# One block of attention and gated FFN on one core: the product with V goes first in its step, the eighth output unit moves to step 6, and five x buffers

## The chip, the cores and the metric

The kernel runs on one core of a Trainium2 chip. A core has five engines that run their own instruction streams and meet at semaphores: TensorE (PE, matrix products into PSUM), VectorE (DVE), ScalarE (ACT), GpSimd (POOL) and SyncE (SP), which here only issues DMAs. The metric is the time of one execution in microseconds (us), lower is better; before the change the median of three runs is 1512.0 us (1510.33 to 1512.47).

## The reference, cut to what matters

```python
# x [2, 1024, 512]; 16 heads of size 128; FFN width 1365
def attn(x):
    q, k, v = (einsum('bsd,hed->bhse', x, W) for W in (W_Q, W_K, W_V))
    scores = where(causal, -1e9, einsum('bhse,bhme->bhsm', q, k) / sqrt(128))
    z = einsum('bhsm,bhme->bhse', softmax(scores), v)
    return einsum('bhse,hde->bsd', z, W_O)
def ffn(x):                       # w1q, w3q, w2q: weights rounded to -s, 0, +s
    return (silu(x @ w1q.T) * (x @ w3q.T)) @ w2q.T
x = x + layernorm(attn(layernorm(x)))
x = x + layernorm(ffn(layernorm(x)))
```

All is float32. Layernorm is over the last axis, and s is the mean of the absolute weights.

## The kernel before, in words

**Stages.** Attention of batch 0 and then of batch 1 fills the time to about 1270 us; the FFN follows. The heads of both batches are counted through: head n runs from 0 to 31, batch b is n // 16. Two heads make a pair g = n // 2, whose V and output weights are handled together; j = n % 2 tells the two apart.

**Steps.** Each head has eight steps i = 0 to 7, one for each tile of 128 queries, 256 steps in all. The last head takes its query tiles in the order 4 to 7, 0 to 3. A step puts this work on TensorE, in this order:
- up to two *units* from the list `fill[i]` (L860);
- if it is a product step, the *product with V* (`values`, L864, matmul at L650): probabilities, transposed, times V for two query tiles. Products m = 0 to 3 of a head are due at its steps 3, 5, 7 and at step 2 of the next head;
- the rest of the units (L867);
- the scores (`scores`, L556) of the query tile three steps ahead.

Units are: a half of the next head's Q or K projection (`query_key_unit`, L471 and L478, 12 matmuls), a quarter of the next pair's V (`value_unit`, L499, 24 matmuls), an output unit, which multiplies the last pair's z with W_O for one token tile (`output_units`, L519, 6 matmuls), a block unit, which transposes a normalised x tile of batch 1 (`block_unit`, L403), and in the last heads transposes for the FFN (L256) and FFN units (`early_hidden`, L318). Output units come in even heads: three at step 0, then one at each of steps 1, 4, 5, 6 and 7. V units come in odd heads, at steps 0, 1, 6 and 7.

**One chain per pair of query tiles.** Scores go to PSUM; VectorE masks the diagonal (L561) and takes the maximum (L565); ScalarE takes the exponential (L572) and, after VectorE's reciprocal (L577), scales it (L578); VectorE turns 32x32 blocks (L604). SP writes the blocks to DRAM ("hop", L615) and reads them back in four DMAs as `pt` (L631), which completes the transpose; the product needs these reads. ScalarE reads the product out twice (L662), VectorE and GpSimd make its low and difference forms (L667, L670).

**Split matmuls.** Projections and output units work on a leading, a low and a difference form of both factors. They write two PSUM tiles, main and diff. ScalarE scales main out (L454 for Q, K and V) and VectorE combines it with diff (L458 for q, L456 for k and v; L530 and L533 for output units, which add into `acc`). Weight forms are made by ScalarE (L439), GpSimd (L440) and VectorE (L446).

**PSUM.** The pool `ps_m` has four tiles that are handed out in turn: two for each projection, V or output unit, one for a product or a transpose. The pool `ps_s` has two, for scores; the transposes of the first batch use it too.

**Order.** The code fixes the order of TensorE's work with `past(newest[0])`. On the other engines a planner orders what the code leaves open; `behind(...)` puts weight forms and side work behind marked instructions. Each engine then runs its stream in that order. The lists `side` hold work beside the steps: loads for the statistics (L148, L354), x loads and normalisation for the second batch (`block_load` L380, `normal_unit` L388), rounding of the FFN weights (L199 to L219), and the middle of the block (L273 to L291). These tiles come from `xpool`.

**Start.** Tiles of x are normalised (L123 on VectorE, L388 on ScalarE), transposed (L403), and split (L407, L408, L409). `busy` (L703) adds transposes of an identity, of no use to the result.

Of the kernel before, what the change touches and what calls it, by code (L numbers as in the profile page):

```python
# [35 lines left out]
def sandwich_kernel(  # L36
# [30 lines left out]
    N = 2 * G  # L67
# [54 lines left out]
    def normalise(dst, src, mv, r, t):  # L122
        return nc.vector.tensor_scalar(  # L123
            dst, src, mv[:, t, 0:1], r[:, t : t + 1], ALU.subtract, ALU.mult
        )
# [212 lines left out]
    with ExitStack() as att:  # L338
# [4 lines left out]
        vpool = att.enter_context(tc.tile_pool(name="v", bufs=2))  # L343
        zpool = att.enter_context(tc.tile_pool(name="z", bufs=ZB))
        qpool = att.enter_context(tc.tile_pool(name="q", bufs=2))
        xpool = att.enter_context(tc.tile_pool(name="x", bufs=3))
        ps_s = att.enter_context(tc.tile_pool(name="ps_s", bufs=2, space=PSUM))


# [28 lines left out]
        def block_load(b, t):  # L378
            normal[b, t] = xt = xpool.tile([P, D], FP, name="xt")
            nc.sync.dma_start(xt, x[b, ts(t, P), :])  # L380

        def normal_unit(b, t):
            if b == 0:
                normal[b, t] = acc[:, t, :]
            xt = normal[b, t]
            if b == 0 and t % 2 == 1:
                return normalise(xt, xt, mv_in[b], r_in[b], t)
            return nc.scalar.activation(  # L388
                xt, xt, AF.Identity, scale=r_in[b][:, t : t + 1],
                bias=shifts[b][:, t : t + 1],  # L390
            )

        def block_unit(b, t):
            k, tl = divmod(t, QT)
            if tl == 0:
                xs[b, k] = [xblocks.tile([P, NC, TB], FR, name="xb") for _ in range(3)]
            xt = normal[b, t]
            if b == 0:
                ps = ps_s.tile([P, NC, P], FP, name="tr", tag="s_ps")
            else:  # L400
                ps = ps_m.tile([P, NC, P], FP, name="tr", tag="mm")
            for c in range(NC):
                newest[0] = nc.tensor.transpose(ps[:, c, :], xt[:, ts(c, P)], ident)  # L403
            lead, low, diff = (form[:, :, ts(tl, P)] for form in xs[b, k])
            eng = nc.vector if b == 0 and tl >= QT // 2 else nc.gpsimd
            return (
                nc.scalar.mul(lead, ps, LEAD / T12),  # L407
                nc.vector.scalar_tensor_tensor(low, lead, -T12, ps, ALU.mult, ALU.add),  # L408
                eng.tensor_tensor(diff, lead, low, ALU.subtract),  # L409
            )  # L410
# [271 lines left out]
        @contextmanager  # L682
        def past(*instructions):
            with ExitStack() as order:
                for i in instructions:
                    order.enter_context(tc.issue_after(i.ins))
                yield
# [10 lines left out]
        def busy(times):  # L698
            with ExitStack() as order:
                if newest[0] is not None:  # L700
                    order.enter_context(past(newest[0]))
                for _ in range(times):
                    newest[0] = nc.tensor.transpose(idle, ident, ident)  # L703
# [4 lines left out]
        with past(*done):  # L708
            for kind in range(2):
                lead_and_low(kind, 0, EVERY, first=True)  # L710
            blocks = []
            for t in range(QT):
                blocks.append(block_unit(0, t))
                if t % 2 == 1:
                    busy((8, 3)[t // 2])
        lead, low, diff = blocks[-1]
        with past(diff):
            for kind in range(2):
# [12 lines left out]
        side = [[] for _ in range(N * NT)]  # L731
        at = 0

        def two_steps_each(pairs, at):
            for first, then in pairs:
                side[at].append(first)
                side[at + 2].append(then)
                at += 2
            return at

        for k in range(3):
            pairs, total, last = mean_abs_units(k, xpool)
            at = two_steps_each(pairs, at)
            side[at + 1].append(total)
            side[at + 3].append(last)
        at = two_steps_each([stats_units(t) for t in range(NT)], at)
        side[at + 1].append(lambda: std_unit(1, 0, NT))

        block_at = 2 * (NP - 1) * NT + 5
        assert at + 1 < block_at - 3  # L750
        for t in range(NT):
            side[block_at - 3 + t].append(lambda t=t: block_load(1, t))
            side[block_at - 2 + t].append(lambda t=t: normal_unit(1, t))
        at += (1 - at) % 4 + 4
        for stages in ternary_steps(qpool):
            for later, stage in zip((0, 2, 3, 4), stages):
# [56 lines left out]
        for n in range(N):  # L813
            g, j = divmod(n, 2)
            b, pr = divmod(g, NP)

            fill = [[] for _ in range(NT)]

            def put(steps, units):
                for i, u in zip(steps, units):  # L820
                    fill[i].append(u)

            if n + 1 < N:
                units = [
                    lambda k=k, kind=kind: query_key_unit(n + 1, kind, k)()
                    for k in range(2)
                    for kind in range(2)
                ]
                late = {2 * NP - 1: (6, 7), N - 2: (5, 5)}.get(n, (5, 6))
                put((3, 4) + late, units)  # L830
            if j == 1 and g + 1 < G:
                units = [lambda u=u: value_unit(g + 1, u) for u in range(QT)]
                put((0, 1, 6, 7) if n != 2 * NP - 1 else (0, 1, 5, 6), units)
            if n == 0:
                put((1, 2), [lambda u=u: value_unit(0, u) for u in (2, 3)])
            if j == 0 and g > 0:
                outs = output_units(g - 1)
                put((0, 0, 0, 1, 4, 5, 6, 7), outs)
            for t in range(NT):
                if divmod(block_at + t, NT)[0] == n:  # L840
                    put([(block_at + t) % NT], [lambda t=t: block_unit(1, t)])
            for t in range(QT):
                if divmod(split_at + t, NT)[0] == n:
                    put([(split_at + t) % NT], splits[t][2:])
            if n == N - 1:
                put((2, 4, 6), [lambda f=f: early_hidden(f) for f in range(EARLY)])
            for i in range(NT):
                idx = n * NT + i
                with behind("turn", of=idx + 1):
                    if n + 2 < N and i > 5:  # L850
                        load_raw(i - 6, n + 2)
                    if j == 0 and g + 1 < G and i == 1 + (n == 0):
                        load_raw(2, g + 1)
                    if j == 1 and i == 1:
                        load_raw(3, g)
                    if n == N - 2 and i >= NT - EARLY:
                        f = i - NT + EARLY
                        load_t13(f, wpool.tile([P, 2, D], FR, name=("va", "vd", "vl")[f]))
                todo = fill[i]
                for u in todo[:2]:  # L860
                    with past(newest[0]):
                        u()
                rest = None
                if idx in product:  # L864
                    with past(newest[0]):
                        rest = values(*product.pop(idx))
                for u in todo[2:]:  # L867
                    with past(newest[0]):
                        u()

                with behind("max", "half", "exp", of=idx + 1):
                    if n + 1 < N and i in (2, 3):
                        difference_form(i - 2, n + 1, EVERY)
                    if n + 1 < N and i in (1, 2):
                        lead_and_low(i - 1, n + 1, EVERY)
                    at = g + 1 - j
                    form_step = i - 3 - (n == 0)
                    if at < G and form_step in (0, 1):
                        lead_and_low(2 + j, at, (FRONT, BACK)[form_step])
                    if at < G and form_step in (2, 3):  # L880
                        difference_form(2 + j, at, (FRONT, BACK)[form_step - 2])
                with past(newest[0]):
                    look(idx + AHEAD)
                if rest:
                    with behind("max"):
                        rest()
                if idx + 2 < len(order):
                    with behind("max"):
                        turn(*order[idx + 2])
                        if idx + 3 == len(order):  # L890
                            bring(*next(iter(blocks_of)))
                with behind("max", "half", "turn"):
                    for u in side[idx]:
                        u()
        outs = output_units(G - 1)
# [7 lines left out]
    with ExitStack() as ffn:  # L903
# [4 lines left out]
        xpool = ffn.enter_context(tc.tile_pool(name="xf", bufs=3))  # L908
# [208 lines left out]
```

## Time and profile before

| what | value |
|---|---|
| median of three runs | 1512.0 us (1510.33 to 1512.47) |
| the profiled execution | 1511.27 us |
| its span, first to last instruction | 1509.5 us |
| granted TensorE clock over the span | 0.997 |
| busy: PE, DVE, ACT, POOL | 98%, 72%, 53%, 27% |
| HBM traffic | 174 GB/s over the span |

All places in time below are microseconds from the start of the span. PE is TensorE's matmuls, PEld its weight loads. A row of a group or of the timeline gives engine, line, operation and tiles (out<-in). In the list of waits, an entry "A <- B" means that A's engine stood idle before A and that B ended it; then come the total, how often, and the longest. Brackets in the timeline give the idle time before an instruction and what ended it. A DMA's row shows the issue by SP; the trace also holds when it landed.

### The profile page before, as it was taken

To read this page: it belongs to the slowest core of one execution; us is meant where nothing else is said; L and a number is where in the kernel's file an instruction comes from. 1 tells how busy PE (TensorE), PEld (TensorE's weight loads), DVE (VectorE), ACT (ScalarE), POOL (GpSimd) and SP (SyncE) were. 2 spreads that over 40 slices of the span, in tenths; PEclk is the share of its full clock that TensorE was granted. 3 is DMA by queue.
4 is the path that set the end of the run, shared out by engine and by line. 5 is a ranking of instruction groups with operands and counts; after the bars stand their busy time and mean duration, and the time that the engine had idled before them with its cause. 6 is when DMAs were issued, how large, how long until landed. Compare 5 with 4: busy or idle time off the path is not lost.

```text
span 1509.5 us, 21335 instructions
## 1 busy us (share of the span) xinstructions
PE 1475.6 (98%) x7061; PEld 1184.9 (78%) x7061; DVE 1080.6 (72%) x2123; ACT 792.7 (53%) x1566; POOL 404.3 (27%) x472
## 2 busy tenths in 40 slices
PE   8999999999999999999999999999999999999997
PEld 6778888887878787777778787878787877888885
DVE  7767686878786878787777777777777776664444
ACT  4656555555555555666664555555555464444332
POOL 3222222222223333434433333333322110210010
PEclk9999999999999999999999999999999999999999
DMA  3666767676666675758866666666665677530200
GB/s 123 194 194 186 195 184 200 185 202 184 201 191 172 181 206 183 205 166 249 238 200 190 195 192 196 195 195 189 179 179 166 181 216 228 176 102 19 91 28 29
DMA packets 179894, 263.57 MB, mean 175 GB/s; under 512 B 19188, under 2 KB 120564, under 8 KB 175688
## 3 DMA queue, kind: packets, MB, share of 16 engines
q1 hardware_dynamic: 179784, 262.20, 59.5%
q8 instruction: 57, 0.93, 0.3%
q14 instruction: 53, 0.43, 0.1%
HBM read 160.43 MB, written 101.71 MB: 174 GB/s over the span
## 4 chain that ended last, share of the span: by engine, by line
PE 66%; issue 10%; DVE 9%; DMA 7%; ACT 5%; POOL 2%; SPq 1%; DVEq 0%; POOLq 0%; ACTq 0%
PE mm L650 11%; PE mm L471 10%; PE mm L318 10%; PE s_ps L556 10%; PE mm L499 8%; PE mm L519 6%; PE yp L933 5%; PE mm L478 5%; DVE nm L565 3%; DMA hop<-blocks 2%; ACT p_sb L572 2%; DMA wqk<-wk 2%; ACT p_sb L578 1%; POOL kl L440 1%; DVE blocks L604 1%
## 5 line engine op out<-in xcount | busy, mean ns | idle before, releaser
L572 ACT ACTIVATE p_sb<-s_ps,nm 128x128 f32<-128x128 f32 (+7 forms) x256 | 190.0, 742 | 367.3 <-DVE nm L565 360.8
L556 PE MATMUL s_ps<-k,q 128*128 128x512 f32 (+3 forms) x768 | 289.7, 486 | 0.7 <-ACT p_sb L572 0.7
L650 PE MATMUL mm<-pt,v_sb 128*128 128x256 f32 (+1 forms) x1280 | 271.7, 359 | 11.3 <-ACT q L454 3.7
L650 PEld LDWEIGHTS mm<-pt,v_sb 128*128 128x128 f32 x1280 | 238.1, 190 | 48.8 <-ACT q L454 6.2
L578 ACT ACTIVATE p_sb<-p_sb,ri 128x128 f32<-128x128 f32 (+7 forms) x256 | 197.7, 773 | 33.0 <-DVE ri L577 30.5
L565 DVE TENSOR_REDUCE nm<-s_ps 128x1 f32<-128x128 f32 (+7 forms) x256 | 193.7, 757 | 7.1
L604 DVE STREAM_TRANSPOSE blocks<-p_sb 128x128 f32<-128x128 f32 (+7 forms) x256 | 197.1, 770 | 1.2 <-ACT p_sb L578 0.9
L556 PEld LDWEIGHTS s_ps<-k,q 128*128 128x128 f32 x768 | 132.3, 190 | 69.4 <-issue 61.4
L670 POOL TENSOR_TENSOR zd<-za,zl 128x256 fp32r<-128x256 f32 x128 | 94.7, 739 | 328.0 <-DVE zl L667 319.7
L561 DVE TENSOR_TENSOR s_ps<-s_ps,causal 128x128 f32<-128x128 f32 x256 | 75.4, 295 | 136.1 <-PE s_ps L556 135.6
L499 PE MATMUL mm<-va,xb 128*128 128x256 f32 x512 | 158.5, 310 | 0.0
L499 PE MATMUL mm<-vd,xb 128*128 128x256 f32 x512 | 144.9, 283 | 0.9 <-POOL xb L409 0.9
L499 PE MATMUL mm<-vl,xb 128*128 128x256 f32 x512 | 144.6, 282 | 0.0
L471 PE MATMUL mm<-xb,qa 128*128 128x512 f32 x256 | 119.6, 467 | 1.0 <-ACT xb L407 1.0
L471 PE MATMUL mm<-xb,ka 128*128 128x512 f32 x256 | 112.3, 439 | 0.0
L499 PEld LDWEIGHTS mm<-vl,xb 128*128 128x128 f32 x512 | 97.7, 191 | 7.1 <-issue 4.1
L499 PEld LDWEIGHTS mm<-va,xb 128*128 128x128 f32 x512 | 97.7, 191 | 7.1 <-issue 3.9
L471 PE MATMUL mm<-xb,ql 128*128 128x512 f32 x256 | 101.7, 397 | 0.0
L471 PE MATMUL mm<-xb,kl 128*128 128x512 f32 x256 | 100.7, 393 | 0.1
L499 PEld LDWEIGHTS mm<-vd,xb 128*128 128x128 f32 x512 | 97.7, 191 | 1.1 <-POOL xb L409 1.1
L601 POOL MEMSET blocks<- 128x128 f32 x128 | 26.2, 205 | 263.1 <-DMA hop<-blocks 185.2
L533 DVE TENSOR_TENSOR acc<-acc,mm 128x512 f32<-128x512 f32 x128 | 86.1, 683 | 12.7 <-ACT acc L528 5.4
(162 smaller groups left out, 2777.3 us busy)
## 6 DMA issues: line engine op xcount, KB each, us to landing
hop<-blocks SPq DMA_DIRECT2D x32, 1024.0 KB, 4.5
pt<-hop SPq DMA_DIRECT2D x128, 256.0 KB, 6.2
hop<-blocks SPq DMA_DIRECT2D x32, 768.0 KB, 3.3
pt<-hop SPq DMA_DIRECT2D x128, 192.0 KB, 3.8
hop<-blocks SPq DMA_DIRECT2D x32, 512.0 KB, 3.2
pt<-hop SPq DMA_DIRECT2D x128, 128.0 KB, 3.2
wqk<-wq SPq DMA_DIRECT2D x32, 256.0 KB, 5.2
wqk<-wk SPq DMA_DIRECT2D x32, 256.0 KB, 6.6
```

The costliest lines, as they stand in the source:

```text
L318: newest[0] = nc.tensor.matmul(ps[:fl, :], lhsT=t[:, c, :], rhs=bl[k][:, c, :], start=(c == 0 and k == 0), stop=(c == NC - 1 and k == 1),)
L471: newest[0] = nc.tensor.matmul(main, lhsT=forms[f][0][:, c, :], rhs=forms[f][1][:, c, :], start=(c == 0 and f == 0), stop=(c == NC - 1 and ...
L499: newest[0] = nc.tensor.matmul((main, main, diff)[f][:, ts(t, 2 * P)], lhsT=forms[f][0][:, c, token], rhs=forms[f][1][:, c, :], start=(t = ...
L519: newest[0] = nc.tensor.matmul((main, main, diff)[f], lhsT=zs[g, t // QT, j][f][:, ts(t % QT, P)], rhs=weights[3, g][f][:, 2 * j : 2 * j + ...
L533: nc.vector.tensor_tensor(dst, dst, diff, ALU.subtract)
L556: newest[0] = nc.tensor.matmul(s_ps[:, ds(k0, kl)], lhsT=proj[n, 0, i // QT][:, ts(i % QT, P)], rhs=proj[n, 1, k0 // TB][:, :kl], start=Tr ...
L565: top = nc.vector.tensor_reduce(nm, s_ps[:, :L], axis=AX.X, op=ALU.max, negate=True)
L572: e = nc.scalar.activation(p_sb[:, :L], s_ps[:, :L], AF.Exp, bias=nm, accum_out=rs)
L578: nc.scalar.mul(p_sb[:, :L], p_sb[:, :L], ri)
L604: turned = nc.vector.transpose(b[:, :, 0 : i + 1, il, :].rearrange("p to t r -> p t to r"), p_sb[:, :L].rearrange("p (b r) -> p b r", r=32),)
L650: newest[0] = nc.tensor.matmul(dst, lhsT=proj[g, 2][:, kt, ts(j, P)], rhs=rhs, start=(kt == 0), stop=(kt == 2 * m + 1),)
L670: nc.gpsimd.tensor_tensor(diff, lead, low, ALU.subtract)
```

## The change

It has these parts:
- In a product step the product with V comes ahead of all units, not behind the first two; in head 30 (`n == N - 2`) two units stay ahead of it.
- The last of the eight output units of an even head moves from step 7 to step 6, which then has a K unit and two output units.
- Loads and normalisation of x tiles for batch 1 come one step earlier, and `xpool` has five tiles instead of three.
- In the start, the transposes of tiles 2 and 3 take tiles of `ps_m`, and the idle transposes behind the first and second pair of tiles are 7 and 8, not 8 and 3.

```diff
-        xpool = att.enter_context(tc.tile_pool(name="x", bufs=3))
+        xpool = att.enter_context(tc.tile_pool(name="x", bufs=5))
...
-            if b == 0:
+            if b == 0 and t not in (2, 3):
                 ps = ps_s.tile([P, NC, P], FP, name="tr", tag="s_ps")
             else:
                 ps = ps_m.tile([P, NC, P], FP, name="tr", tag="mm")
...
-                    busy((8, 3)[t // 2])
+                    busy((7, 8)[t // 2])
...
-            side[block_at - 3 + t].append(lambda t=t: block_load(1, t))
-            side[block_at - 2 + t].append(lambda t=t: normal_unit(1, t))
+            side[block_at - 4 + t].append(lambda t=t: block_load(1, t))
+            side[block_at - 3 + t].append(lambda t=t: normal_unit(1, t))
...
-                put((0, 0, 0, 1, 4, 5, 6, 7), outs)
+                put((0, 0, 0, 1, 4, 5, 6, 6), outs)
...
-                for u in todo[:2]:
+                front = 2 if n == N - 2 else 0
+                for u in todo[:front]:
                     with past(newest[0]):
                         u()
                 rest = None
                 if idx in product:
                     with past(newest[0]):
                         rest = values(*product.pop(idx))
-                for u in todo[2:]:
+                for u in todo[front:]:
```

More of the change, by code (lines that the diff above doesn't have):

```diff
@@ L749, in sandwich_kernel @@
         block_at = 2 * (NP - 1) * NT + 5
-        assert at + 1 < block_at - 3
+        assert at + 1 < block_at - 4
         for t in range(NT):
-            side[block_at - 3 + t].append(lambda t=t: block_load(1, t))
-            side[block_at - 2 + t].append(lambda t=t: normal_unit(1, t))
+            side[block_at - 4 + t].append(lambda t=t: block_load(1, t))
+            side[block_at - 3 + t].append(lambda t=t: normal_unit(1, t))
         at += (1 - at) % 4 + 4
```

## The prediction

> **What bounds the kernel now.** I read the page's busy times first, then busy time by stretch, then TensorE's waits.
>
> ```profile
> PE 1475.6 (98%) x7061; PEld 1184.9 (78%) x7061; DVE 1080.6 (72%) x2123; ACT 792.7 (53%) x1566; POOL 404.3 (27%) x472
> ```
>
> ```profile
> 300.00:400.00 100.00, 100.00 (x484) 79.92 (x484) 78.55 (x162) 54.77 (x115) 24.33 (x34) 1.00 0.67 193
> ...
> 700.00:800.00 100.00, 96.83 (x472) 76.81 (x471) 71.84 (x146) 61.85 (x125) 41.16 (x44) 1.00 0.76 225
> ```
>
> Columns after the stretch and its length: busy us of TensorE (PE), its weight loads, VectorE, ScalarE and GpSimd, the granted clock, DMA share, GB/s. TensorE is the bound; from 100 to 500 us it never pauses. Both builds hold the same instructions on every engine, except four more idle transposes, so the product matmuls cost the same and only TensorE's pauses can change. The skill speaks against trusting that figure: "Perfetto Trace Analysis", "Identifying the Most-Contended Engine", calls matmul busy share a poor measure of headroom and takes weight-load busy share, here 78%. By that rule a new order might win a part of the other 22%. By the rows it can't: following 128x512 matmuls of a projection start 227 to 233 ns apart whatever is ahead of them, and the long first one of a unit (630 ns) follows a score recorded as 28 ns, which together is the two normal lengths. I take the rows: the pauses are all there is.
>
> ```profile
> PE mm L650 <- ACT q L454: 3.7, 6, 0.9
> PE mm L650 <- DVE acc L530: 3.2, 2, 1.7
> PE tr L403 <- ACT acc L388: 2.8, 3, 1.2
> PE mm L650 <- DMA pt<-hop: 2.7, 3, 1.9
> PE mm L478 <- ACT q L454: 2.2, 2, 1.6
> PE tr L403 <- DVE xb L408: 1.8, 1, 1.8
> PE tr L403 <- ACT xt L388: 1.6, 2, 1.3
> ```
>
> The timeline places them: the product (L650) waits at step 5 of even heads from 14 on (1.65, 1.51, 0.73, then 0.52 to 0.87 us in heads 20 to 28) for a PSUM tile that ScalarE has yet to read; L403 waits at 11 us and 612 us; the DMA waits are in the last head.
>
> **First 31 us.** Transposes of tiles 2 and 3 no longer wait 1.83 us (till 10.97) for VectorE to release a score tile. Their input is ready at 9.72 (ScalarE L388, 8.90 + 0.81). ScalarE finishes the leads of tiles 0 and 1 at 10.68, those of 2 and 3 then at about 11.8; VectorE's low forms (0.64 each) end at 12.8 instead of 13.59. VectorE works on with no real pause through the difference forms (kd till 19.26) and the statistics, and TensorE waits for these at 24.63, so **0.8 us** goes. The four extra transposes (0.11 each, 0.44) lie in the wait for these leads; without that cover they cost 0.4.
>
> ```profile
> 12.90:16.40 3.50, 3.48 (x8) 2.53 (x9) 3.50 (x5) 1.00 (x2) 3.50 (x3) 0.53 0.29 117
> ```
>
> Here the granted clock (0.53) halves the first projections: 428 ns apart instead of 230. "TensorE: Matmul & The Clock Gate", Part 1, says that the clock is halved until some 3.4 us of steady activity, so closing the pause could save nearly 8 x 0.2 = 1.6 us. By the rows it saves none: kd is ready at 19.26, long after these matmuls. I count 0.8 (0 to 1.5). Five x buffers let two more weight pieces (233 KB each) load ahead of the first W_O, Q and K loads on SP's queue, at 407 GB/s some 1.2 us, hidden: these are needed after 30 us.
>
> **Blocks of the second batch (heads 14, 15).** Loads and normalisation come a step earlier: the two waits for L388 go, -1.6. In head 14 the product's 1.65 goes too, but the transposes after it then need the tile that q's combine reads, behind 0.8 (L388) and 1.1 (L578) on ScalarE; I put +0.4 for what is not regained. Net **-1.2** (-3.2 to +0.5). Head 16: its 1.51 is lost again at the wait of its last product, **0**.
>
> **Product first.** It starts earlier by the unit it passes: 2.76 us for a Q/K unit at steps 3 and 5, 2.87 for a V unit at step 7. It needs the four reads of the transposed probabilities. From each product's start, less the landing the trace records for its last read and less the unit passed, what is left is 2 to 5 us mostly, but 0.2 to 1.1 at step 3 of heads 1, 5, 7, 11, 17, 19, 23, 25, 27 and 29, and negative in two places: -1.5 at step 7 of head 17 (start 723.44, landing 721.88) and -1.2 at step 3 of head 18. Behind a waiting product stands all of TensorE, and through it the score that feeds VectorE. GpSimd's zd (L670) moves a few places in a queue that is busy 27%: nothing.
>
> The built order also moves ScalarE's work. Head 24 before, ScalarE then VectorE:
>
> ```profile
> 973.29 0.90 ACT L572 ACTIVATE p_sb<-s_ps,nm 128x768 f32<-128x768 f32 x1 [2.33 <-DVE nm L565]
> 974.10 0.19 ACT L572 ACTIVATION_READ_ACCUMULATOR p_sb<-s_ps,nm 128x1 f32 x1
> 974.19 0.59 ACT L454 ACTIVATE q<-mm 128x512 f32<-128x512 f32 x1
> 974.67 0.93 ACT L578 ACTIVATE p_sb<-p_sb,ri 128x768 f32<-128x768 f32 x1
> ...
> 976.02 0.65 ACT L439 ACTIVATE va<-wvo 128x512 fp32r<-128x512 f32 x1
> ```
>
> ```profile
> 974.81 0.69 DVE L458 SCALAR_TENSOR_TENSOR q<-mm,q 128x512 f32<-128x512 f32 x1 [0.32 <-ACT q L454]
> ...
> 975.74 1.09 DVE L565 TENSOR_REDUCE nm<-s_ps 128x1 f32<-128x896 f32 x1
> ```
>
> In the changed build L454 stands behind L439 and L578: 0.65 + 0.93 = 1.58 us later. VectorE's L458 waits for it, and behind that the maximum (L565), the turns (L604) and the hop write. Following head 24 row by row, its last turn (till 989.34) ends some 1.25 later; the write goes out right after it (989.41), so the reads, landed at 1002.96, land at about 1004.2. The product that starts at 1003.36 would by then start 0.5 earlier, as step 5's wait is gone: about 1.5 us of waiting, net +1.0. The same sum by head, with slacks of 4.5, 1.8, 0.4, 0.8, 3.2 us: heads 20, 22, 24, 26, 28 give -0.5, +0.9, +1.1, +0.7, -0.5, **+1.7** (-2 to +6). In the first batch VectorE has pauses there that take the delay up.
>
> Head 17: the combine is 0.75 + 0.62 + 0.93 = 2.3 later (two L662 pass it too), so reads land at 723.7; TensorE arrives at 720.4, waits 3.4 and still has the V unit before it: +3.4. Head 18 then starts late enough to lose its waits of 0.56 and 0.73. With 0.5 for head 19, **+2.6** (-1 to +5).
>
> **Eighth unit.** Its six matmuls (1.36 us) move from step 7 to 6; nothing is gained by itself. Three units in a row want six of four PSUM tiles; in head 24 VectorE would release the last (L456) at 991.4, wanted at 991.2: 0. But W_O's load (512 KB), which needs that unit done, goes ahead of the last-quarter reads in SP's queue in heads 2, 4, 6 and 8, whose slacks are 3.0, 0.6, 1.6 and 1.4; 512 KB at 193 GB/s is 2.7 us, partly spent by then: **+0.5** (0 to 2.5).
>
> **Last head.** Here products also go ahead of the FFN units (L318):
>
> ```profile
> 1246.96 4.20 PE L318 MATMUL mm<-xb,vl 128*128 128x512 f32 x16
> 1253.04 3.48 PE L650 MATMUL mm<-pt,v_sb 128*128 128x256 f32 x16 [1.88 <-DMA pt<-hop]
> ```
>
> FFN units cover the reads now. The first product's reads land at 1235.50: TensorE would wait from 1232.4. The third's land at 1252.9, perhaps 1.3 sooner, as ScalarE no longer loads the Silu table (1.28) before that softmax. From about 1252.2: product 3.4, FFN unit 4.0, product 0.8, four output units 5.5, the last product begins at 1265.9 instead of 1263.74: **+2.2** (0.4 to 4).
>
> **Sum.** -0.8 - 1.2 + 0 + 2.6 + 1.7 + 0.5 + 2.2 = +5.0 us on the profiled execution, 1511.27 (span 1509.5, 1.8 around it unchanged): 1516.3. The median, 1512.0, is 0.7 above it: **1517**.
>
> **Rivals.** *Faster, the waits for PSUM simply go:* if ScalarE's new order costs nothing because VectorE is waiting for scores anyway, heads 14 to 28 lose 1.65 + 1.6 + 1.51 + 0.56 + 0.73 + 2.97 = 9.0 and the start 0.8; with 1.5 for head 17 and 2.2 for the end, -6: **1506**. It decides where L458 waits under 0.5 us in heads 20 to 28. For it: first-batch slack is 3.7 us. Against: VectorE is behind in the second batch (it came to that maximum late, after 2.79 us for GpSimd).
> *Nothing to see:* reads are early nearly everywhere, gains and the end cancel: **1511**, 1509 to 1514. For it: no pause at all in 100 to 500.
> *The chain slips everywhere:* if the 1.5 us delay reaches the reads in every head, some fourteen places with slack below 1.1 wait about 1 us each: **1525**. Against it: first-batch VectorE pauses, such as 1.9 us ahead of a mask (L561) in head 2.
>
> **How the numbers follow.** A measurement of this kernel can tell about 0.2%, 3 us. Forecast 0.50 (own range 1513.5 to 1521, of which 0.08 lies within 3 us), nothing to see 0.20, faster 0.13, slips everywhere 0.17. So faster 0.13, same 0.28, slower 0.59. The range 1507.5 to 1525.5 leaves out most of the fastest case and a third of the slowest.
>
> **What would show it.** Right: L403's wait near 11 us gone and kd formed near 18.5; step 5's waits gone; L458 waiting over 1 us for L454 in heads 20 to 28; DMA waits of L650 grown from 2.7 to 10 us or more, the largest in head 17 and the last. Wrong: L650 hardly waits for DMA outside the last head, or waits for PSUM move to L478 and L519. Wrong too if SP's altered order brings reads sooner than the old slacks say.

## The result, and the profile after

| | before | changed |
|---|---|---|
| median | 1511.65 us (1510.33 to 1512.47, 4 runs) | 1531.8 us (1530.93 to 1533.54, 4 runs) |
| ratio, 95% interval | | 1.0136 (1.0118 to 1.0153) |
| profiled execution, its span | 1511.27, 1509.5 us | 1533.54, 1531.3 us |

The change costs 20.2 us. The forecast was 1517.0 in a range to 1525.5: the sign was right, the size four times too small. The page of the changed kernel, busy times first:

```profile
PE 1486.7 (97%) x7065; PEld 1188.1 (78%) x7065; DVE 1068.5 (70%) x2123; ACT 791.3 (52%) x1566; POOL 400.7 (26%) x472
```

Busy time by stretch (length, then TensorE, weight loads, VectorE, ScalarE, GpSimd, granted clock, DMA share, GB/s):

```profile
300.00:400.00 100.00, 100.00 (x490) 79.43 (x489) 75.34 (x157) 54.24 (x114) 25.83 (x34) 1.00 0.69 199
700.00:800.00 100.00, 93.20 (x437) 73.19 (x437) 67.16 (x142) 61.20 (x120) 41.35 (x43) 0.98 0.74 219
```

From the list of waits, one row of VectorE, two of TensorE and one of its weight loads:

```profile
DVE q L458 <- ACT q L454: 47.0, 35, 2.2
...
PE mm L650 <- DMA pt<-hop: 11.3, 12, 3.4
...
PE mm L478 <- ACT zf L662: 5.2, 3, 2.6
...
PEld mm L519 <- DVE acc L530: 4.6, 12, 0.4
```

TensorE's recorded pauses grew from 24.1 to 34.9 us in all, and that is only half of it. Its busy time grew by 11.1 us too, though it runs the same matmuls and only four more transposes of 0.11 us. So "the pauses are all there is", on which the forecast stood, fails. Two causes make most of the 11.1 us of busy time.

**Half clock behind pauses.** Four times before TensorE's work ends, the granted clock falls to half in the changed kernel's trace, each time for 3.41 us and behind a pause. The rows are in pairs: the 3.41 us ahead of a fall, and the stretch behind it.

```profile
74.79:78.20 3.41, 1.36 (x7) 0.90 (x6) 2.64 (x5) 1.53 (x5) 1.26 (x2) 1.00 0.80 239
78.20:81.70 3.50, 3.50 (x10) 2.77 (x9) 0.34 (x2) 1.29 (x3) 1.27 (x1) 0.51 0.52 165
614.10:617.51 3.41, 1.57 (x14) 1.37 (x13) 3.38 (x6) 1.31 (x4) 2.63 (x3) 1.00 1.07 285
617.70:621.10 3.40, 3.40 (x15) 2.96 (x15) 1.41 (x4) 1.69 (x3) 0.00 (x0) 0.53 0.88 321
726.74:730.15 3.41, 1.10 (x5) 0.93 (x6) 1.75 (x5) 2.29 (x6) 2.98 (x3) 1.00 0.85 234
730.30:733.60 3.30, 3.30 (x17) 3.30 (x17) 3.21 (x8) 1.35 (x4) 0.74 (x1) 0.51 0.41 103
1252.39:1255.80 3.41, 0.87 (x4) 0.82 (x5) 2.40 (x5) 2.44 (x5) 0.00 (x0) 1.00 0.92 288
1256.20:1259.60 3.40, 3.40 (x10) 2.68 (x10) 1.13 (x1) 0.66 (x2) 1.47 (x2) 0.56 0.64 122
```

TensorE is fully busy in the second row of each pair, at a clock of 0.51 to 0.56. Compared step by step with the kernel before, the steps concerned lose 1.5 to 1.8 us beyond their pauses, 6.8 us together. Before, there was one such stretch, from 13.1 us on. It is gone now, and that saved nothing: kd, for which TensorE waits next, is formed at 19.14 us where it was 19.26.

The falls lie on a grid. In each of the 14 traces all changes of the clock are whole multiples of 3.413 us apart (here 78.20, 617.51, 730.15 and 1255.80: 158, 33 and 154 of them), and where the grid lies in the span differs from execution to execution. In the four windows ahead of the falls TensorE was busy for 0.40, 0.46, 0.32 and 0.25 of the time.

**Delays of one matmul that are no pause on record.** The row "PEld mm L519 <- DVE acc L530" stands at 0.4 us, once, before, and at 4.6 us, 12 times, now. Compared step by step, the third output unit puts step 0 of twelve even heads 0.23 to 0.25 us back, 2.8 us in all. The timeline in head 10, VectorE and then TensorE, first of the kernel before and then of the changed one:

```profile
412.20 0.65 DVE L530 SCALAR_TENSOR_TENSOR acc<-mm,acc 128x512 f32<-128x512 f32 x1
...
413.26 0.62 PE L519 MATMUL mm<-oa,za 128*128 128x512 f32 x2
```

```profile
417.36 0.65 DVE L530 SCALAR_TENSOR_TENSOR acc<-mm,acc 128x512 f32<-128x512 f32 x1
```

```profile
417.49 0.61 PE L519 MATMUL mm<-od,zd 128*128 128x512 f32 x2
418.06 0.73 PE L519 MATMUL mm<-oa,za 128*128 128x512 f32 x2
```

L530 reads the first output unit's main tile until 418.01, and the third unit, which gets that tile again, starts at 418.06. Before, the same L530 ended 0.41 us ahead of its matmul. V's combine (L456, 0.69 us) now comes right ahead of these units on VectorE, since the V unit is no longer followed by a product of 2.4 us.

A wait of the product also costs more than its recorded pause: behind nine waits of the changed kernel the step lost some 0.24 us more, and five waits at step 5 (heads 20 to 28), when they went, gave back 0.21 to 0.27 us more. The net is about 1 us.

**Where the 21.8 us of span go.** I took the scores of query tile 1 of an even head in each trace (step 6 of the head before issues them), as that is the same point of the work in both, and subtracted their time before. The columns are heads; the last is the span.

| kernel | 2 | 6 | 10 | 14 | 16 | 18 | 20 | 28 | end |
|---|---|---|---|---|---|---|---|---|---|
| changed | 2.5 | 3.9 | 4.7 | 5.9 | 9.7 | 14.3 | 14.9 | 16.2 | 21.8 |
| e1, product first alone | 0.6 | 1.7 | 2.3 | 4.1 | 7.2 | 9.9 | 12.3 | 11.4 | 14.4 |
| e2, all but product first | 0.5 | 0.9 | 0.8 | 0.8 | 4.7 | 4.7 | 4.9 | 4.9 | 5.7 |
| e7, buffers and early loads | -0.2 | 0.1 | 0.1 | 0.1 | 5.7 | 5.7 | 5.8 | 6.0 | 6.4 |
| e5, step 5 of even heads | 0.4 | 0.4 | 0.5 | 0.5 | 3.0 | 2.8 | 3.3 | 0.2 | 0.7 |
| e8, step 3 | 2.8 | 2.9 | 2.9 | 3.0 | 5.2 | 8.4 | 9.7 | 12.3 | 11.4 |
| e9, step 7 | -0.1 | 2.0 | 2.5 | 3.5 | 4.7 | 5.9 | 6.5 | 7.4 | 8.3 |
| e12, last head | 0.2 | 0.2 | 0.2 | 0.2 | -0.3 | 0.1 | 0.1 | 0.1 | 3.5 |

Each row is one profiled execution; the verdicts below are medians. How much one execution may differ where nothing is changed shows at head 2: the pause at 77 us was 1.04 us before, 1.52 in e12 and 2.02 in e11, three programs that are the same up to that point. The rows also hold half clock: after the start the profiles of before, e4 and e6 have none, the changed kernel's has four stretches, and the others one or two places each, near 617 us in e1, e2 and e7, for example.

### The profile page after: what moved, and what is told of

It is laid out like the page before. It is cut to its first block, busy times and chain, and to the rows that moved or that the text cites. A ratio compares the mean times of both kernels' runs of the same rounds, so it can differ in the third digit from the quotient of the medians.

```text
span 1531.3 us, 21286 instructions
## 1 busy us (share of the span) xinstructions
PE 1486.7 (97%) x7065; PEld 1188.1 (78%) x7065; DVE 1068.5 (70%) x2123; ACT 791.3 (52%) x1566; POOL 400.7 (26%) x472
## 4 chain that ended last, share of the span: by engine, by line
PE 63%; DMA 11%; DVE 11%; issue 7%; ACT 5%; POOL 1%; SPq 1%; DVEq 0%; POOLq 0%; ACTq 0%
PE mm L318 10%; PE mm L471 10%; PE mm L650 10%; PE s_ps L556 10%; PE mm L499 7%; PE mm L519 6%; DMA hop<-blocks 6%; PE yp L934 5%; PE mm L478 5%; DMA pt<-hop 2%; DVE nm L565 2%; DMA wqk<-wk 2%; DVE blocks L604 2%; ACT p_sb L572 1%; ACT p_sb L578 1%
## 5 line engine op out<-in xcount | busy, mean ns | idle before, releaser
L650 PEld LDWEIGHTS mm<-pt,v_sb 128*128 128x128 f32 x1280 | 241.8, 192 | 62.8 <-issue 20.9
L650 PE MATMUL mm<-pt,v_sb 128*128 128x256 f32 (+1 forms) x1280 | 275.3, 362 | 12.0 <-DMA pt<-hop 11.3
L556 PEld LDWEIGHTS s_ps<-k,q 128*128 128x128 f32 x768 | 136.8, 190 | 74.1 <-issue 61.7
L471 PE MATMUL mm<-xb,ka 128*128 128x512 f32 x256 | 112.1, 438 | 0.9 <-ACT q L454 0.9
L471 PE MATMUL mm<-xb,qa 128*128 128x512 f32 x256 | 106.6, 416 | 0.7 <-ACT xb L407 0.7
L456 DVE TENSOR_TENSOR v_sb<-v_sb,mm 128x512 f32<-128x512 f32 x64 | 43.8, 684 | 86.9 <-ACT v_sb L454 86.9
L471 PE MATMUL mm<-xb,ql 128*128 128x512 f32 x256 | 100.7, 393 | 0.4 <-DVE xb L408 0.4
L471 PE MATMUL mm<-xb,kl 128*128 128x512 f32 x256 | 100.7, 393 | 0.0
```

The source lines that it names most:

```text
L471: newest[0] = nc.tensor.matmul(main, lhsT=forms[f][0][:, c, :], rhs=forms[f][1][:, c, :], start=(c == 0 and f == 0), stop=(c == NC - 1 and ...
L556: newest[0] = nc.tensor.matmul(s_ps[:, ds(k0, kl)], lhsT=proj[n, 0, i // QT][:, ts(i % QT, P)], rhs=proj[n, 1, k0 // TB][:, :kl], start=Tr ...
L650: newest[0] = nc.tensor.matmul(dst, lhsT=proj[g, 2][:, kt, ts(j, P)], rhs=rhs, start=(kt == 0), stop=(kt == 2 * m + 1),)
```

## The experiments

Times are medians, each against the kernel before run beside it (1512.1 to 1512.3 us).

**e1, product first alone.**

```diff
-                for u in todo[:2]:
+                front = 2 if n == N - 2 else 0
+                for u in todo[:front]:
...
-                for u in todo[2:]:
+                for u in todo[front:]:
```

> The kernel before, with the product ahead of a step's other units (all heads but N-2) and nothing else of the change. Theory A (the new order of TensorE alone costs the time: it meets the reads of the transposed probabilities and the PSUM tiles that products still hold, and three of its pauses are followed by some 3.4 us at half clock): +17 to +21 us, so 1529 to 1533, with the pauses before the product in heads 0, 4, 17 and 30 there again. Theory B (earlier loads, the fifth x buffer and the eighth unit shift SP's queue and so make the reads late; the order only shows it): at most +10, near 1520. What was predicted for these steps (+1.5, +2.6, +1.7, +2.2, less 1.65 in head 14): +6 to +8.

Measured 1525.71 us, ratio 1.0098 (1.0083 to 1.0113): +13.6, between the theories. The order of TensorE is two thirds of the loss, not all of it. Of the pauses named, that for head 4's last quarter did not come back (no pause over 0.25 us there); those of the other heads did.

**e2, all but product first** (`front = 2` in the changed kernel).

> The changed kernel with the old order within a step (two units, product, rest): so the fifth x buffer, tiles 2 and 3 through the other PSUM pool, the earlier loads and the eighth unit alone. Theory A: -2 to +2 us against the kernel before, 1510 to 1514; the two waits for L388 near 600 us gone, the start the same within 0.3 us. Theory B: +8 us or more, with waits of the product for the reads in several heads.

Measured 1518.14 us, ratio 1.0042 (1.0028 to 1.0055): +6.0. Neither theory had it. Most of the loss is in one place, between heads 14 and 16, where TensorE paused 4.67 us, with half clock behind it until 620.78. With e1 it adds up to 13.6 + 6.0 = 19.6 of 20.2, but this is no proof that the two leave each other alone: e10 shows that they do not.

**e3, the eighth unit alone** (the put list ends in 6, 6).

> The kernel before with the eighth output unit at step 6 and nothing else. Theory A: within 1 us of the kernel before (predicted +0.5). Theory B: W_O's load goes ahead of the last reads in SP's queue and the product waits there in heads 2, 4, 6, 8: +3 us or more.

Measured 1512.8 us, ratio 1.0006 (0.9998 to 1.0015). The predicted +0.5 stands within what can be told; the unit alone is not the cause.

**e4, the changed kernel with the old order in the last head.**

```diff
-                front = 2 if n == N - 2 else 0
+                front = 2 if n >= N - 2 else 0
```

> The changed kernel with the old order within a step in the last head too (as it already has in head N-2). In the changed kernel's trace the last head loses 9 us against before: a pause of 3.4 us before its first product, 1.9 us more in the half-clock stretch behind it, and what follows. Theory A: 7 to 9 us faster than the changed kernel, 1523 to 1525, and the half-clock stretch near 1256 us gone. If instead only the pause itself counts and the clock is a bystander: 3 us faster, 1529. What was predicted of this step: 2.2 faster.

Measured 1526.29 us, ratio 1.0104 (1.0087 to 1.0121): 5.5 faster than the changed kernel, less than expected. Its profile told more than its time: it has the same pauses as the changed kernel, 3.06 us at 78.38, 1.83 at 616.66, 2.58 at 727.39, and no half clock behind any of them:

```profile
73.65:77.06 3.41, 1.67 (x9) 1.00 (x8) 2.57 (x6) 1.75 (x5) 1.37 (x1) 1.00 1.07 279
77.06:80.47 3.41, 2.10 (x10) 1.89 (x11) 1.40 (x4) 2.12 (x4) 1.43 (x2) 1.00 0.20 61
79.00:82.40 3.40, 3.40 (x17) 2.77 (x16) 0.00 (x0) 0.91 (x3) 1.14 (x1) 1.00 0.46 150
...
725.60:729.01 3.41, 1.62 (x9) 1.45 (x10) 1.72 (x6) 2.18 (x4) 2.86 (x2) 1.00 0.90 222
728.00:731.40 3.40, 3.40 (x28) 3.31 (x27) 3.37 (x8) 1.35 (x4) 1.31 (x2) 1.00 0.44 109
```

So a pause of 1.8 to 3.4 us may or may not be followed by half clock, and the difference between these two profiles (7.0 us) is largely that: in these three places half clock cost the changed kernel 5.0 us. The grid tells which: e4's is placed so that an edge (77.06, 616.37, 725.60) cuts each of the three pauses in two, and the emptiest windows still have TensorE busy for 0.49, 0.49 and 0.47. Over all windows of the 14 traces that are at full clock, up to the end of TensorE's work, the 13 with a busy share below 0.43 were all followed by half clock, of the 22 from 0.43 to 0.51 13 were, and of those above none was.

**e5, product first at step 5 of even heads alone.**

```diff
+                front = 0 if j == 0 and i == 5 else 2
```

> The kernel before, with the product first at step 5 of even heads alone, where before it waits for a PSUM tile in heads 14 to 28. Theory C (product first costs at steps 3 and 7, where it meets the reads and leaves its PSUM tile to the next output units; at step 5 it only gains): the waits of 0.52 to 0.87 us in heads 18 to 28 go, those of heads 14 and 16 come back at the output unit behind; -2 to -4 us, 1508 to 1510. Theory D (the combine of q that ScalarE now does later slips the chain of reads wherever the order is changed): the gain is eaten up, -1 to +3 us.

Measured 1511.26 us, ratio 0.9995 (0.9987 to 1.0004): no change that can be told. The trace agrees with theory C all the same: from head 20 to 28 it gains 3.1 us, and it loses 2.5 between heads 14 and 16, where its profile has a half-clock stretch behind a pause of 1.88 us.

**e6, five buffers alone** (`bufs=5`).

> The kernel before with five x buffers in place of three and nothing else. In the run without product first the product of head 0's last quarter waited 1.86 us at 77 us instead of 1.04 and the last head lost 1 us. If the fifth buffer alone does this (weight pieces are loaded in pairs, ahead of other loads in SP's queue): +0.5 to +2 us. If it is hidden, as predicted: within 0.5 us of the kernel before.

Measured 1511.79 us, ratio 0.9998 (0.999 to 1.0006): hidden, as predicted.

**e7, five buffers and the earlier loads and normalisation.**

```diff
-            side[block_at - 3 + t].append(lambda t=t: block_load(1, t))
-            side[block_at - 2 + t].append(lambda t=t: normal_unit(1, t))
+            side[block_at - 4 + t].append(lambda t=t: block_load(1, t))
+            side[block_at - 3 + t].append(lambda t=t: normal_unit(1, t))
```

> The kernel before with five x buffers, and the second batch's loads and normalisation one step earlier. Predicted for the earlier step: the two waits for L388 near 612 us go, -1.6 us. Theory E (ScalarE's L388 now stands behind a softmax exp and division in its queue, for which it waits, as in the run without product first, where TensorE paused 4.67 us at 617 us): +3 to +5 us, of which 2.8 to 4 between heads 14 and 16, with a pause over 3 us before L403.

Measured 1516.67 us, ratio 1.003 (1.0018 to 1.0041): +4.3, theory E. TensorE and then ScalarE in its timeline:

```profile
617.15 1.11 PE L403 MATMUL tr<-ident,xt 128*128 128x128 f32 x4 [4.67 <-ACT xt L388]
```

```profile
611.99 0.59 ACT L407 ACTIVATE xb<-tr 128x512 fp32r<-128x512 f32 x1
614.45 0.80 ACT L572 ACTIVATE p_sb<-s_ps,nm 128x640 f32<-128x640 f32 x1 [1.88 <-DVE nm L565]
615.15 0.19 ACT L572 ACTIVATION_READ_ACCUMULATOR p_sb<-s_ps,nm 128x1 f32 x1
615.57 0.83 ACT L578 ACTIVATE p_sb<-p_sb,ri 128x640 f32<-128x640 f32 x1 [0.23 <-DVE ri L577]
616.30 0.80 ACT L388 ACTIVATE xt<-xt,shift,r_in 128x512 f32<-128x512 f32 x1
```

The x tile had landed at 611.79 (its load was issued at 602.72), so L388 could have run at 612.58, when ScalarE fell idle. It stands behind an exponential that waits for a maximum, and behind that one's division, and comes 3.7 us later. The step that was to take a wait away did so for the tile before (its L403 runs at 610.80, without the pause of 1.27 us) and built the largest pause of the trace for this one: normalisation asked for earlier came out later in ScalarE's stream. The pause is only part of the cost: the window ahead of 616.35 was empty, the clock was halved for two windows behind it, and the step lost 2.95 us beyond its pauses.

```profile
616.35:623.18 6.83, 6.03 (x16) 4.91 (x17) 1.29 (x2) 3.79 (x7) 4.04 (x5) 0.50 0.65 204
```

**e8, product first at step 3 alone** (`front = 0 if i == 3 and n < N - 2 else 2`).

> The kernel before with the product first at step 3 alone, in heads 0 to 29. Theory C: here the product passes a Q/K unit of 2.76 us, and the slack of its reads before was 3.1 to 4 us in heads 17, 19, 23, 25, 27, 29: +1 to +5 us, in waits of the product for the reads in odd heads. Theory D: the combine of q is 1.58 us later in every head, so reads land 1 us or more later than before in all heads, and the products that were not moved (last quarter, step 2) wait too, in heads 5, 11, 17, 29: +5 us or more.

Measured 1519.36 us, ratio 1.0046 (1.0034 to 1.0058): +7.0, and both theories missed its form. Between heads 2 and 14 it loses 0.1 us: no slip of the chain, no late reads in odd heads, although VectorE's L458 waits 30.0 us for L454 in the whole trace in place of 6.6 (in heads 2 to 13 it waits over 1 us in three places only, from 467 us on). What grew are the waits for PSUM at step 5, in its list of waits against 3.7 and 3.2 us before:

```profile
PE mm L650 <- ACT q L454: 6.2, 6, 1.0
...
PE mm L650 <- DVE acc L530: 4.0, 2, 2.2
```

The product that was moved here makes another step's product wait longer: 1.04 us in place of 0.52 to 0.87 in each of heads 20 to 28. Its profile also has half clock behind the pauses at 77.8 and 594 us, and most of the rest goes in heads 17 to 19.

**e9, product first at step 7 alone** (`i == 7`).

> The kernel before with the product first at step 7 alone, in heads 0 to 29. In the changed kernel's trace the third output unit of an even head's first step starts 0.12 to 0.23 us late, in twelve of fourteen heads, with no pause on record; the step-3 and step-5 runs do not show it. Theory F (the product that goes ahead of the V unit holds the PSUM tile which the third output unit wants, and gives it back after ScalarE's two reads; before, the V unit's tile was wanted there): 0.25 us a pair of heads, 3 us, and head 17 loses 2 to 4 us at its last step as in the changed kernel: +4 to +7 us. If the delay comes from the eighth unit or the buffers: within 1 us outside head 17.

Measured 1521.73 us, ratio 1.0066 (1.0053 to 1.008): +9.6, more than expected. Its list of waits has the output unit's row, 13 times:

```profile
PE mm L650 <- DMA pt<-hop: 5.6, 4, 2.0
PEld mm L519 <- DVE acc L530: 5.0, 13, 0.4
```

The place of theory F is right and its mechanism wrong: the tile is not one that the product holds (in the changed kernel's head 10, ScalarE's reads of it end at 412.66, 5 us earlier) but the first output unit's, held by VectorE's L530. The largest single loss is a pause of 1.5 us for the reads in head 5. They were issued when they were before (219.05 against 219.04 us) and landed 1.8 to 2.0 us later, behind a weight piece (L148) loaded 0.5 us ahead of them; before, it went 3.2 us ahead. That this load delays them is argued, not shown.

**e10, the changed kernel with the old steps of loads and normalisation.**

> The changed kernel with the second batch's loads and normalisation back at their old steps. If the earlier step costs here what it costs alone (4.3 us, in one pause of 4.67 us before L403): 3 to 4 us faster than the changed kernel, 1528. If product first already moves these waits (the run with product first alone lost 3.1 us between heads 14 and 16 with the old steps, the changed kernel 3.8): within 1.5 us of the changed kernel, 1530.5 to 1532.

Measured 1530.91 us, ratio 1.0117 (1.0104 to 1.013): 0.9 faster than the changed kernel, within what can be told. What costs 4.3 us alone costs next to nothing on top of product first, which moves the waits at 600 to 620 us by itself. So e1 and e2 add up because two differences cancel: without the early loads the change still costs 18.8 us, 5.2 more than product first alone (e1), and the parts left in it, the eighth unit and the buffers, cost +0.7 and -0.6 alone; the start was not run alone.

**e11, product first at step 5 of heads 20 to 28 alone.**

```diff
+                front = 0 if j == 0 and i == 5 and n >= 20 else 2
```

> The kernel before with the product first at step 5 of heads 20, 22, 24, 26 and 28 alone. In the run with step 5 of all even heads, these five heads gained 3.1 us against before, and heads 14 to 18 lost what they gained. Theory C: -2.5 to -3.5 us, 1509, faster than the kernel before and the changed one. Theory D: 0 or slower.

Measured 1509.57 us (22 runs), ratio 0.9983 (0.9977 to 0.999): 2.6 us faster than the kernel before, the fastest of all. Five products lose their wait at step 5, and only in head 28 another takes its place in part (0.33 us ahead of L471). One row of the product for L454 is left in its list of waits, that of head 18:

```profile
PE mm L650 <- ACT q L454: 0.7, 1, 0.7
```

**e12, product first in the last head alone** (`front = 0 if n == N - 1 else 2`).

> The kernel before with the product first in the last head alone. Predicted for this step: +2.2 (0.4 to 4), with TensorE waiting for the first reads from 1232 to 1235.5 us. From the changed kernel's trace, a half-clock stretch may follow that pause and make it +4. If the last head's 9 us in the changed kernel come from this step: +7 or more.

Measured 1516.4 us, ratio 1.0026 (1.002 to 1.0032): +4.2. Its profile has a pause of 2.92 us until 1235.52 (expected: 1232 to 1235.5), half clock behind it, and loses 3.5 us from there on.

## Why the prediction was wrong in size

By its own steps, in us; "alone" is a median, "together" is read from the table of heads:

| step | predicted | alone | together |
|---|---|---|---|
| first 31 us | -0.8 | | -0.1 |
| heads 0 to 13 | 0, eighth unit +0.5 | e3 +0.7, rest not zero | +6.0 |
| loads and normalisation earlier, heads 14, 15 | -1.2 | e7 +4.3 | +3.8 |
| heads 16 to 19 | +2.6 | | +5.2 |
| heads 20 to 29 | +1.7 | | +2.5 |
| head 30, last head | +2.2 | e12 +4.2 | +4.4 |
| sum | +5.0 | | +21.8 span, +20.2 median |

- **"The pauses are all there is": failed.** This is the first step that failed. The weighing of weight-load share against matmul starts was right as far as it went (of the 26 steps 3 and 5 of heads 1 to 13, whose order alone changed, 24 kept their length within 0.02 us), but busy time also hides half-clock stretches and delays too short to be recorded: 6.8 and 2.8 us, against 1.6 for the stretch at 13.1 us that is gone, and 1 for what waits cost beyond their pauses; some 2 us of the 11.1 I could not place. The other half, 10.8 us, is pauses, where the terms of heads 0 to 13, 14 to 19 and the last head were wrong or too small. Half clock was weighed at the start only, where it is free, though the forecast itself put pauses of about 3 us into heads 17 and 31.
- **First 31 us: mechanism right, gain not there.** L403's wait near 11 us went, and VectorE finished the low forms 1.0 us earlier. But kd was formed at 19.14, not near 18.5 as the prediction asked, because VectorE's two L409 took longer. The timelines before and after:

```profile
13.51 2.37 DVE L409 TENSOR_TENSOR xb<-xb 128x512 fp32r<-128x512 f32 x2
```

```profile
12.53 3.23 DVE L409 TENSOR_TENSOR xb<-xb 128x512 fp32r<-128x512 f32 x2
...
12.24 2.98 POOL L409 TENSOR_TENSOR xb<-xb 128x512 fp32r<-128x512 f32 x2
```

The last row is GpSimd's, in the changed kernel. VectorE's first L409 took 0.68 us before and 1.54 now, when it began just behind one of GpSimd's. The Trainium skill, "GPSIMD Engine Reference", Specifications, says that the two engines share their SBUF interfaces and contend when VectorE has two SBUF inputs, as here. The rows agree: what was gained ahead of the shared stretch was handed back in it. The durations of before could not be carried over to a new overlap.
- **Heads 0 to 13 at zero: failed.** "From 100 to 500 us it never pauses" was read as room. Of the 6.0, 2.6 lie in the pause at 77 us with its half clock, which is partly chance (how long the pause was, and how the grid fell on it); 1.2 are five of the late output units; 1.9 are waits for reads in heads 5, 7 and 11.
- **Loads and normalisation earlier: wrong sign.** The working moved L388 one step ahead as if ScalarE's stream followed the step. It does not; e7 shows the row. Together with product first the sign could not be told (e10): the +3.8 is nearly all product first's, which loses 3.1 us in these heads without the earlier step (e1).
- **Heads 17 to 19: direction right, size off, and another wait.** The DMA wait of 3.4 us at step 7 of head 17 did not come. (The forecast's own figures for it do not meet: a landing at 721.88, made 2.3 later, is 724.2 and not 723.7.) TensorE paused 2.59 us at step 6, in the second Q/K unit behind the product (L478), for the product's PSUM tile which ScalarE read out (L662) only behind a division of 1.15 us; half clock behind the pause cost 1.8 us more:

```profile
727.30 1.15 ACT L578 ACTIVATE p_sb<-p_sb,ri 128x1024 f32<-128x1024 f32 x1 [0.46 <-DVE ri L577]
728.36 0.36 ACT L662 ACTIVATE za<-mm 128x256 fp32r<-128x256 f32 x1
728.62 0.37 ACT L662 ACTIVATE zf<-mm 128x256 f32<-128x256 f32 x1
```

"Waits for PSUM move to L478 and L519" had been named as what would make the prediction wrong; it is a part of it (5.2 and 1.5 us).
- **Heads 20 to 29: right.** The waits at step 5 went, L458 waits 1.67 us for L454 in each of these heads (predicted 1.58), and the net is +2.5 (predicted +1.7), of which 1.2 are the late output units that the forecast did not have. By even head and the odd one behind it: -0.4, +0.9, +0.6, +0.1, +1.3, where -0.5, +0.9, +1.1, +0.7, -0.5 was predicted. In all heads L458's wait grew from 6.6 to 47.0 us.
- **Eighth unit, five buffers: right**, +0.7 and -0.6 alone.
- **Last head: mechanism right, size off.** The term is +4.2 alone where +2.2 was summed; the half clock behind the pause is the part that was left out. The end of the wait came within 0.1 us in e12. In the changed kernel 2.0 us of TensorE's pauses here are waits of the FFN's transposes (L256) for VectorE; e2 has them too, e1, e3, e6 and e7 do not, so it takes two parts of the change together or the start, which no run separates.
- **DMA waits of L650** grew from 2.7 to 11.3 us, as predicted (10 or more), the largest (3.43) in the last head.
- **The rivals.** "The chain slips everywhere", 1525, came nearest and is still 7 us short. Its mechanism fails in heads 2 to 13: in the changed kernel L458 waits over 1 us for L454 in ten places there, and the product waits for late reads in heads 5, 7 and 11 alone (1.9 us). The faster rival is true for five heads: e11.

What stays open: the parts of product first that were run cost 19.7 us alone (-1.1, +7.0, +9.6, +4.2), and all of it together 13.6; step 5 of odd heads was never run alone. In heads 14 to 18 and behind the pause at 77 us the parts meet the same waits, but which part saves which was not separated. Nor is it known which of the eighth unit, the buffers and the start costs the 5.2 us on top of product first. How often a pause is followed by half clock was seen in one profile of each kernel only.

## What to carry to other kernels

An engine that never pauses for 400 us need not have slack: look for delays in start-to-start times and in the rows of its weight loads, not only in its pauses. Where a planner orders the other engines, asking for work a step earlier can put it later in the stream; read that stream in the built kernel before giving the step a sign. A move that helps in some steps and hurts in others is worth making where it helps: product first at step 5 of heads 20 to 28 wins 2.6 us, everywhere it loses 13.6.

## What the runs showed of the hardware

A pause of TensorE far shorter than the half-clock stretch is enough to start one: 1.83 us was followed by 3.4 us at 0.53, while 2.58 and 3.06 us in another execution were followed by none. What decides is how much of the pause falls into one window of the execution's grid: a window of 3.413 us with a recorded busy share below 0.43 was always followed by half clock, one above 0.51 never, and between the two both happened. An estimate from these shares: with TensorE busy otherwise, a single pause under 1.6 us starts none, one over 3.9 us always does, and between them it is the place on the grid that decides. The Trainium skill, "TensorE: Matmul & The Clock Gate", Part 1, puts the clock back after an idle window of about 3.4 us, and has the windows run freely. The length of the stretches and the grid here agree with it; that the window must be idle does not: of the 26 falls in the 14 traces only those of e2 and e7 near 617 us came behind an empty one.
